# Three to five buffers for messages and one-hot columns, one wait per quad, and first layers two steps apart, in a graph layer on one Trainium2 core

## The chip, the core and the metric

The kernel runs on one core of a Trainium2 chip, in one launch. Its metric is the device time of that launch in microseconds (us). Five engines work side by side, each through its own queue in order, and they wait for one another by semaphores: TensorE (PE, with its weight loads shown as PEld), VectorE (DVE), ScalarE (ACT), GpSimd (POOL) and SyncE (SP). DMA transfers are issued from the queues of SP, ACT and POOL. A wait at the head of a queue holds back all that stands behind it in that queue.

## What is computed

The reference is one layer of a graph network with a layer norm behind it: 12500 nodes of 128 features, 400000 edges sorted by destination, all in 32-bit floats.

```python
rbf = jnp.exp(-(distances[:, None] - centers) ** 2 / (2.0 * width * width))
cut = 0.5 * (jnp.cos(jnp.pi * distances / CUTOFF) + 1.0) * (distances <= CUTOFF)
W = (jax.nn.silu(rbf @ fw1 + fb1) @ fw2 + fb2) * cut[:, None]
messages = (h[src] @ pw + pb) * W
agg = jax.ops.segment_sum(messages, dst, num_segments=num_atoms)
out = h + (jax.nn.silu(agg @ mw1 + mb1) @ mw2 + mb2)
x = _layernorm(x + out)
```

An edge beyond the cutoff gives nothing. The kernel therefore packs the edges that count into a dense list first, and works on that list.

## The kernel before

The packed list is worked through in 139 **quads** (NL) of 512 edges, four tiles of 128 edges each. Two neighbouring quads are an **oct**. The list is made in seven chunks, by DVE instructions for the most part, which run between the first quads. Meanwhile PE projects all node features to the table `proj` in memory. POOL then gathers the projected rows of the edges' sources, four gathers per quad (L1101), into one of the quad buffers. From quad 70 on, the work on the nodes (second network, residual, norm, store) runs between the quads.

One step q of the main loop (L1595 to L1648) does, in this order of code:

- `message(q)`: one DVE product (L1203) of the second layer's result, in a PSUM bank, with the gathered quad. Its output is a `msg` buffer.
- `second(q + 2)`: PE's second layer for the quad after next, a bias matmul (L1184) and four matmuls (L1187), which read `s` and write a PSUM bank. There are four such banks, and a message sets one free.
- `first(o)` and `silu(o)` in two steps of every four: PE's first layer of a whole oct (L1169, four records) into `ph`, which has one buffer, and ACT's activation from `ph` to `s` (L1175). `octs(q)` says which oct. `s` has three buffers.
- in step 4m+3, `basis(o)` for two octs: on ACT a square (L1153) and an exponential (L1157) into `rbf`, which has two buffers.
- `sum_up(q, msg)`: PE adds the messages up by destination (L1237). Each of the four tiles is multiplied with a one-hot matrix, a column of `hot` in the code's words, into the PSUM tile `sums`.
- `place(q + 1)`: DVE makes the next quad's four one-hot columns (L1216), one instruction for each.
- in some steps `add`: DVE adds earlier sums to the table `aggT` (L1271).

POOL's gathers are paced: a gather of quad q waits until a numbered DVE instruction is done, by the table PACE. So POOL's pace hangs on DVE's.

`own` gives out the buffers of messages and one-hot columns. Quad q has the buffer q % 2 of each kind, and from OWN_4 = 66 the buffer q % 4, with two of each kind in quad buffers that are free by then (OTHERS). So before quad 66 the columns of place(q + 1) overwrite what sum_up(q - 1) read, and each of the four columns waits for its own matmul of that sum.

Some source rows are fetched one by one on ACT's queue (`one_row`, L1077, into `row_sb`), for four quads (BY_ACT). `beside` hides a few of these issues behind each activation.

The integer zeros `zero_i`, 376 words wide, clear the packed list in memory, by DMAs on SP's queue (L229).

Of the kernel before, what the change touches and what calls it, by code (L numbers as in the profile page):

```python
# [21 lines left out]
P = 128  # L22
# [4 lines left out]
W = 128  # L27
# [26 lines left out]
MASK_0 = 4  # L54
LATER = 63, (0, 1, 2, 3, 8, 9, 10, 11, 12)
OTHERS = 4, 5, 6, 7
OWN_4 = 66
DIRECT = 32
FIRST = 16
LISTS = 5  # L60
# [27 lines left out]
TAIL = {80: 4, 84: 4, 88: 2, 90: 2, 92: 2, 94: 2, 96: 2}  # L88
LOAD_AT = {80: 12, 84: 11, 88: 10, 90: 9}
NODES = 70  # L90


@with_exitstack
def kernel(
# [122 lines left out]
    nc.gpsimd.iota(iota_i, pattern=[[1, WS]], base=0, channel_multiplier=0)  # L217
    part_i = keep.tile([P, 1], I32, name="part_i")
    nc.gpsimd.iota(part_i, pattern=[[0, 1]], base=0, channel_multiplier=1)
    zero_i = keep.tile([P, 376], I32, name="zero_i")  # L220
    packed = dram.tile([LISTS, MW], I32, name="packed")

    def clear_packed(k, eng):
        a, b = CLEAR[k:k + 2]
        for i in range(LISTS if k == 0 else 3):
            v = packed[i, a:b].rearrange("(p w) -> p w", p=P)
            for w0 in range(0, (b - a) // P, 376):
                n = min(376, (b - a) // P - w0)
                eng.dma_start(v[:, w0:w0 + n], zero_i[:, :n])  # L229

    aggT = keep.tile([P, N], F32, name="aggT")

    to_clear = [(n0, min(n0 + WS, N)) for n0 in range(0, N, WS)]

# [599 lines left out]
    def unpack(c):  # L834
# [110 lines left out]
        yield 0  # L945
        mine = [q for q in SINGLY if QB[c] <= q < QB[c + 1]]
        if mine:
            at_row = work.tile([64, P], I32, name="at_row", bufs=3)
            nc.vector.tensor_scalar(at_row[:np_], f_src[:, :P], float(4 * H), None, op0=OP.mult)
            for q in mine:  # L950
                p = 2 * (q - QB[c])
                singles[q in BY_ACT].extend((q, e, at_row[p:p + 1]) for e in range(P))
# [78 lines left out]
    d_of, rbf_of, ph_of, t_of, s_of, pu_of, got_of, pa_of, hot_of = ({} for _ in range(9))  # L1031


    row_sb = nc.alloc_sbuf_tensor("row_sb", [P, 5, H], F32).ap()

    def own(q, name, also):

        k = q % (4 if q >= OWN_4 else 2)
        if k > 1:
            return quad_sb[OTHERS[2 * also + k - 2]]  # L1040
        if (name, k) not in own_sb:
            own_sb[name, k] = keep.tile([P, QT, H], F32, name=f"{name}{k}")
        return own_sb[name, k]

    own_sb = {}
    singles, alone, regs, row_at = ([], []), {}, {}, [0.0]
    ROW_SEMS = 3
    row_sem = [[tc.alloc_semaphore(f"rows{k}_{i}") for i in range(ROW_SEMS)] for k in range(2)]
# [16 lines left out]
    def one_row(act):  # L1065

        eng, of, n = (nc.scalar, BY_ACT, ACT_AT_ONCE) if act else (nc.sync, BY_SP, AT_ONCE)
        q, e, i = singles[act].pop(0)
        k = of.index(q)
        if e == 0:  # L1070
            alone[q] = row_sb[:, 3 + k % 2, :] if act else row_sb[:, k % 3, :]
        if e % n == 0:
            _, regs[act] = nc.values_load_multi_w_load_instructions(
                i[:, e:e + n], engines=[eng.engine], min_val=0,
                max_val=(N - 1) * 4 * H, skip_runtime_bounds_check_because=
                "sources are at most N - 1 where they are copied")
        row = eng.dma_start(alone[q][e:e + 1, :].bitcast(U8),  # L1077
                            proj.rearrange("n f -> (n f)").bitcast(U8)[ds(regs[act][e % n], 4 * H)]
                            .rearrange("(o f) -> o f", o=1))
        on_own(row, row_sem[act][k % ROW_SEMS], "rows")  # L1080
# [83 lines left out]
    def first(o):  # L1164

        rbf, n = rbf_of.pop(o)
        ph = ps.tile([P, 2, QE], F32, name="ph", bufs=1)
        for h in range(n):
            nc.tensor.matmul(ph[:, h, :], w1_sb[:2 * KR, h, :], rbf[:2 * KR], start=True, stop=True)  # L1169
        ph_of[o] = ph, n  # L1170
# [40 lines left out]
    def place(q):  # L1211

        hot = own(q, "hot", 1)
        for j in range(QT):
            at = 2 * q + j // 2, slice(j % 2, j % 2 + 1)
            nc.vector.tensor_scalar(hot[:, j, :wide(q)], iota_n[:, :wide(q)], dl[:, at[0], at[1]],  # L1216
                                    cut[:, at[0], at[1]], op0=OP.is_equal, op1=OP.mult)
            gathers()
        hot_of[q] = hot

    def wide(q):

        return WIDE_0 if q < DIRECT // QT else WIDTHS[chunk_of(q)]
# [5 lines left out]
    def sum_up(q, msg, js=range(QT)):  # L1229
        hot = hot_of[q]  # L1230
        if q % 2 == 0 and 0 in js:
            pa_of["two"] = ps.tile([P, 2, 2 * W], F32, name="sums", bufs=2)
        pa = pa_of[q] = pa_of["two"][:, q % 2, :]
        n = QT // windows(q)
        for j in js:
            k = j // n
            nc.tensor.matmul(pa[:, k * W:k * W + wide(q)], msg[:, j, :], hot[:, j, :wide(q)],  # L1237
                             start=(j % n == 0), stop=(j % n == n - 1))

    bases = {}  # L1240

# [346 lines left out]

    def octs(q):

        return q // 4 * 2 + 2 + q % 4


    some, counted = None, []
    for q in range(NL - 7):  # L1595
        while todo and q + 2 >= DIRECT // QT and todo[0] <= chunk_of(min(q + 2, NQ - 1)):
            go_on(todo[0])
        msg = message(q)
        nodes(q)
        most[0] = room(q)  # L1600
        fetches(clock[0], most[0])
        fetches(math.inf, min(NL, q + AHEAD + 1))
        gathers()
        assert fetched[0] > QT * min(NL - 1, q + AHEAD)
        if q >= CLEAR_Q:
            clear()
        if loads_later and q >= 8:
            nc.sync.dma_start(*loads_later.pop(0))
        radials(q // 2 + 5)
        one_by_one()  # L1610
        multiplies(q + 1 + EARLY_X)
        if q + 2 < NL:
            second(q + 2)
        if q % 4 < 2 and 2 * octs(q) < NL:
            first(octs(q))
            silu(octs(q))
        if q % 4 == 3:
            for o in (q // 4 * 2 + 4, q // 4 * 2 + 5):
                if 2 * o < NL and q < NL - 8:
                    basis(o)  # L1620
        sum_up(q, msg)
        now = range(added(q), added(q + 1))
        at_once = len(now) == 2 and wide(now[0]) == wide(now[1]) and windows(now[0]) == windows(now[1])
        if at_once:
            bases_of(list(now))
        else:
            for k in now:
                base_of(k, (0,))
        place(q + 1)
        for k in now:  # L1630
            if not at_once:
                base_of(k, (1,))
            add(k)
        tail(q)
        clock[0] = max(clock[0], there_at[q])
        summed[q] = clock[0] + 0.7
        clock[0] += 2.2 + 0.3 * (windows(q) - 1)
        if q == 0:
            clear_packed(2, nc.sync)
        if todo:  # L1640
            pack_until(max(there_at[q + 1], clock[0] + (PACK_US if known[0] >= QB[3] else EARLY_US)), NC_)
        if NODES - 8 <= q < NODES - 2:
            part_of(*(("mb1", mb1_f) if q < NODES - 5 else ("mb2", mb2_f)), (q - NODES + 8) % 3)
        if not todo and not counted:
            counted.append(q)
            count()
        elif counted and some is None and fetched[0] >= QT * NL and not queue:
            some = nc.values_load(bad_i[0:1, 2:3], min_val=0, max_val=3 * E)  # L1648
# [29 lines left out]
    node_stats(80, last_st[:, 4:])  # L1678
    bases_of(list(range(q, NL)))
    place(q + 1)  # L1680
    for o in (octs(q), octs(q + 1)):
        basis(o)
    add(q)
    normal(1)
# [2 lines left out]
    house(q)  # L1687
    msg = message(q)
    second(q + 2)
    first(octs(q - 1))  # L1690
    silu(octs(q - 1))
    sum_up(q, msg)
    place(q + 1)
    node_stats(84, last_st[:, 8:])
# [5 lines left out]
    house(q)  # L1700
    msg = message(q)
    second(q + 2)
    first(octs(q - 1))
    silu(octs(q - 1))
    sum_up(q, msg)
    node_second(88)
    place(q + 1)
# [189 lines left out]
```

## Time and profile before

| | |
|---|---|
| time, median of three runs | 939.34 us (937.1 to 951.75) |
| the profiled execution's own time | 938.97 us |
| its span in the profile | 937.3 us |
| granted TensorE clock, mean | 0.818 |
| DMA, over the span | 91.30 MB, 97 GB/s |
| PE busy | 661.8 us, 71% of the span |
| DVE busy | 563.3 us, 60% |
| POOL busy | 537.4 us, 57% |
| ACT busy | 402.3 us, 43% |

No engine is busy all the time, and what a change is worth must be read from the waits between engines. In a row of waits, the name after the arrow is the engine and line that came last. Where it says "remote", the wait ended by a semaphore that the profile does not put down to an instruction; where it says "issue", the profile shows nothing that was waited for. In a row of the timeline, the first number is the start in us from the span's start, the second the duration, and the bracket the idle time of that engine before it. The quads' stretches are read from the message rows: quad 12 at 233.4 us, quad 66 at 496.3 us, quad 138 at 924.7 us. So 230 to 492 us is the stretch of the packed chunks with two buffers, and 492 to 930 us that with four.

### The profile page before, as it was taken

What the parts mean: (1) busy time and instruction counts of PE and PEld (TensorE: products, weight loads), DVE (VectorE), ACT (ScalarE), POOL (GpSimd) and SP (SyncE); (2) the same over time, 40 slices, a digit from 0 to 9 for tenths busy, and PEclk for the clock granted to TensorE, in tenths of its full rate; (3) what the DMA queues carried; (4) which work ended last, traced back from release to release, by engine and by line L of the source; (5) the groups of instructions that cost most, each with busy time, mean ns of one, the idle gap of its engine ahead of it and who ended that gap; (6) DMA issues with size and microseconds to landing.
All of it is one profiled execution on the core that took longest, in us unless ns stands there. A gap on an engine that the chain in (4) does not pass through costs nothing. (4 is left out here: it accounts for less than half of the span.)

```text
span 937.3 us, 12780 instructions
## 1 busy us (share of the span) xinstructions
PE 661.8 (71%) x3531; PEld 516.3 (55%) x3531; DVE 563.3 (60%) x1733; ACT 402.3 (43%) x567; POOL 537.4 (57%) x573
## 2 busy tenths in 40 slices
PE   4666746557877766776776987679777675966775
PEld 4565535345656644564554666456565454644554
DVE  8367639726878567757677785455554443632546
ACT  4443713215334444634444435345533642544335
POOL 6356546455656565666666555655576566653661
PEclk9688667859889878978988788788897798877789
DMA  7477412323224222232324223431422342233222
GB/s 244 149 238 215 152 42 72 77 55 83 69 81 122 65 71 78 79 91 77 104 65 138 60 64 80 117 108 55 141 71 65 93 136 69 65 93 94 67 76 75
DMA packets 52199, 91.30 MB, mean 97 GB/s; under 512 B 13376, under 2 KB 19616, under 8 KB 52122
## 3 DMA queue, kind: packets, MB, share of 16 engines
q0 software_dynamic: 17968, 37.03, 15.9%
q1 hardware_dynamic: 22868, 35.09, 11.2%
q10 hardware_dynamic: 11286, 18.31, 6.2%
q8 instruction: 29, 0.48, 0.2%
q14 instruction: 48, 0.39, 0.1%
HBM read 74.59 MB, written 15.79 MB: 96 GB/s over the span
## 5 line engine op out<-in xcount | busy, mean ns | idle before, releaser
L1101 POOL DMA_INDIRECT quad<-proj,srci x409 | 389.4, 952 | 275.8 <-issue 92.5
L1187 PEld LDWEIGHTS bank<-fw_sb,s 128*128 128x128 f32 x1112 | 177.1, 225 | 100.8 <-issue 92.5
L1187 PE MATMUL bank<-fw_sb,s 128*128 128x128 f32 x1112 | 181.2, 310 | 29.9 <-issue 29.7
L1175 ACT ACTIVATE s<-ph 128x1024 f32<-128x1024 f32 x70 | 71.2, 1018 | 260.2 <-remote 121.5
L1169 PE MATMUL ph<-rbf,w_sb 102*128 102x512 f32 x278 | 157.1, 693 | 31.8 <-ACT s L1175 28.5
L1216 DVE TENSOR_SCALAR hot<-iota_n,dl,cut 128x80 f32<-128x80 f32 (+4 forms) x408 | 110.6, 337 | 110.8 <-PE sums L1237 64.2
L1237 PEld LDWEIGHTS sums<-hot,msg 128*128 128x128 f32 x816 | 116.1, 210 | 64.8 <-issue 40.8
L1237 PE MATMUL sums<-hot,msg 128*128 128x80 f32 (+4 forms) x816 | 118.5, 292 | 23.4 <-DVE msg L1203 14.8
L1101 POOL DMA_INDIRECT x<-proj,srci x95 | 90.9, 957 | 63.4 <-DVE hot L1216 22.0
L1271 DVE TENSOR_TENSOR aggT<-aggT,sums 128x80 f32 (+4 forms) x209 | 53.8, 257 | 108.8 <-remote 44.5
L1169 PEld LDWEIGHTS ph<-rbf,w_sb 102*128 102x128 f32 x278 | 55.7, 223 | 80.1 <-issue 43.8
L1184 PE MATMUL bank<-fb_b,ones_b 96*128 96x512 bf16 x139 | 59.8, 430 | 51.7 <-DVE msg L1203 19.7
L350 PEld LDWEIGHTS bank<-pw_sb,xT 128*128 128x128 f32 (+1 forms) x292 | 49.5, 242 | 51.2 <-issue 32.5
L1203 DVE TENSOR_TENSOR msg<-bank,quad 128x512 f32<-128x512 f32 (+1 forms) x78 | 52.9, 678 | 33.5 <-remote 9.7
L1237 PE MATMUL sums<-quad,quad 128*128 128x128 f32 (+3 forms) x296 | 51.7, 319 | 23.3 <-issue 18.3
L1237 PEld LDWEIGHTS sums<-quad,quad 128*128 128x128 f32 x296 | 48.0, 237 | 27.6 <-issue 21.8
L1101 POOL DMA_INDIRECT quad<-in_x_dram,srci x48 | 47.1, 981 | 24.1 <-issue 13.1
L1153 ACT ACTIVATE rbf<-d_sb,rbf_bias,rbf_scale 102x512 f32<-102x512 f32 x70 | 56.2, 803 | 9.2 <-issue 7.2
L350 PE MATMUL bank<-pw_sb,xT 128*128 128x128 f32 (+1 forms) x292 | 50.5, 329 | 8.1 <-ACT xT L1007 4.8
L1175 ACT ACT_TABLE_LOAD x35 | 44.9, 1283 | 23.3 <-issue 22.9
L1157 ACT ACTIVATE rbf<-rbf 102x512 f32<-102x512 f32 x70 | 44.1, 630 | 17.3 <-issue 15.9
L1203 DVE TENSOR_TENSOR quad<-bank,quad 128x512 f32<-128x512 f32 (+2 forms) x40 | 25.6, 641 | 41.7 <-PE bank L1187 14.3
(281 smaller groups left out, 834.4 us busy)
## 6 DMA issues: line engine op xcount, KB each, us to landing
d_sb<-near_d ACTq DMA_DIRECT2D x67, 256.0 KB
x<-in_x_dram SPq DMA_DIRECT2D x46, 256.0 KB
row_sb<-proj ACTq DMA_DIRECT2D x512, 0.5 KB
quad<-proj,srci POOLq DMA_INDIRECT x409
proj<-hp SPq DMA_DIRECT2D x24, 256.0 KB
out_dram<-x SPq DMA_DIRECT2D x22, 256.0 KB
x<-proj,srci POOLq DMA_INDIRECT x95
r_d<-in_edge_weight_dram SPq DMA_DIRECT2D x5, 256.0 KB
```

Source lines behind the costliest of these rows:

```text
L350: nc.tensor.matmul(to[:m, k, :], lT[:, k * P:k * P + m], w, start=False, stop=(k == a + c - 1))
L1101: g = nc.gpsimd.indirect_dma_start(out=got[:, j, :], out_offset=None, in_=proj if table is None else table, in_offset=bass.IndirectOffsetO ...
L1153: a = nc.scalar.activation(rbf[:u], d[:u], AF.Square, bias=rbf_bias[:u], scale=rbf_scale[:u])
L1157: nc.scalar.activation(rbf[:u], rbf[:u], AF.Exp, scale=-1.0 / (2.0 * width * width))
L1169: nc.tensor.matmul(ph[:, h, :], w1_sb[:2 * KR, h, :], rbf[:2 * KR], start=True, stop=True)
L1175: nc.scalar.activation(s[:, :n], ph[:, :n], AF.Silu)
L1184: nc.tensor.matmul(pu, ones_b[:, :P], bias_b["fb2"].rearrange("k j f -> k (j f)"), start=True, stop=False)
L1187: nc.tensor.matmul(pu[:, j * H:(j + 1) * H], s[:, j * P:(j + 1) * P], fw2_sb, start=False, stop=(j == QT - 1))
L1203: nc.vector.tensor_mul(msg[:, a:b, :], pu_of[q].rearrange("p (j f) -> p j f", j=QT)[:, a:b, :], got_of[q][:, a:b, :])
L1216: nc.vector.tensor_scalar(hot[:, j, :wide(q)], iota_n[:, :wide(q)], dl[:, at[0], at[1]], cut[:, at[0], at[1]], op0=OP.is_equal, op1=OP.mult)
L1237: nc.tensor.matmul(pa[:, k * W:k * W + wide(q)], msg[:, j, :], hot[:, j, :wide(q)], start=(j % n == 0), stop=(j % n == n - 1))
L1271: nc.vector.tensor_add(to, to, pa[:, k * W:k * W + wide(q)])
```

## The change

It has three edits that belong to it and a few that make room for them.

1. `own` has three buffers, and from quad 66 (now OWN_5) five. Two of the five are the quad buffers of before.
2. In `place`, only the first of a quad's columns waits for PE, namely for the last matmul that read this buffer (`read_by`). The matmuls that no one waits for one by one no longer signal. With three buffers, place(q + 1) overwrites what sum_up(q - 2) read, one step longer ago.
3. `octs(q)` is q // 2 + 2, and a first layer stands in each even step, 4m and 4m+2, where it stood in 4m and 4m+1. The tail has the same two octs at the same places, by LAST_OCTS.
4. For room, `row_sb` has two buffers where five were laid out (the four quads on ACT used two of them), `at_row` has two where it had three, and `zero_i` is a slice of `aggT`, which is cleared later.

```diff
-OWN_4 = 66
+OWN_5 = 66
+LAST_OCTS = 68, 69
...
-    zero_i = keep.tile([P, 376], I32, name="zero_i")
+    aggT = keep.tile([P, N], F32, name="aggT")
+    zero_i = aggT[:, N - 1000:N - 624].bitcast(I32)
...
-            at_row = work.tile([64, P], I32, name="at_row", bufs=3)
+            at_row = work.tile([64, P], I32, name="at_row", bufs=2)
...
-    row_sb = nc.alloc_sbuf_tensor("row_sb", [P, 5, H], F32).ap()
+    row_sb = nc.alloc_sbuf_tensor("row_sb", [P, 2, H], F32).ap()
...
-        k = q % (4 if q >= OWN_4 else 2)
-        if k > 1:
-            return quad_sb[OTHERS[2 * also + k - 2]]
+        k = q % (5 if q >= OWN_5 else 3)
+        if k > 2:
+            return quad_sb[OTHERS[2 * also + k - 3]]
...
-            alone[q] = row_sb[:, 3 + k % 2, :] if act else row_sb[:, k % 3, :]
+            alone[q] = row_sb[:, k % 2, :]
...
-            nc.vector.tensor_scalar(hot[:, j, :wide(q)], iota_n[:, :wide(q)], dl[:, at[0], at[1]],
-                                    cut[:, at[0], at[1]], op0=OP.is_equal, op1=OP.mult)
+            i = nc.vector.tensor_scalar(hot[:, j, :wide(q)], iota_n[:, :wide(q)], dl[:, at[0], at[1]],
+                                        cut[:, at[0], at[1]], op0=OP.is_equal, op1=OP.mult).ins
+            if id(hot) in read_by:
+                tc.declare_no_dep(i, group="sums", keep=[read_by[id(hot)]] if j == 0 else [],
+                                  reason="a quad's first column waits for the last product")
+                if j == 0:
+                    tc.add_manual_dep(i, read_by[id(hot)].name, mybir.DependencyInfo(
+                        mybir.DependencyClass.Sync, mybir.DependencyReason.DATA))
...
-            nc.tensor.matmul(pa[:, k * W:k * W + wide(q)], msg[:, j, :], hot[:, j, :wide(q)],
-                             start=(j % n == 0), stop=(j % n == n - 1))
+            i = nc.tensor.matmul(pa[:, k * W:k * W + wide(q)], msg[:, j, :], hot[:, j, :wide(q)],
+                                 start=(j % n == 0), stop=(j % n == n - 1)).ins
+            if not tc.in_control_flow:
+                tc.add_to_no_dep_group("sums", i)
+                read_by[id(hot)] = i
...
-        return q // 4 * 2 + 2 + q % 4
+        return q // 2 + 2
...
-        if q % 4 < 2 and 2 * octs(q) < NL:
+        if q % 2 == 0 and 2 * octs(q) < NL:
```

What stands in a row on DVE is the same before and after; only the waits differ. In the third chunk, between quads 24 and 46, DVE's rows of two steps are before (in brackets what a row waits for; `x4` stands for four like it; the rows of L541 to L551 are packing, and `msg`, `hot` and `quad` are buffers):

```order
L541 COPY_PREDICATED r_d<-bank_169,r_d 128x510
L547 TENSOR_SCALAR bank_170<-nodes 128x512
L551 SCALAR_TENSOR_TENSOR nodes<-bank_170,nodes 128x512 [waits DVE_49]
L1203 TENSOR_TENSOR msg_1078<-bank_167,quad_76 128x512 [waits DMASW5_49,DMASW6_49,DMASW4_49,DMASW3_49]
L1216 TENSOR_SCALAR hot_1111<-iota_n,dl,cut 128x80 [waits PE_49] x4
L541 COPY_PREDICATED nodes<-bank_170,nodes 128x508 [waits DVE_49]
L541 COPY_PREDICATED r_d<-bank_170,r_d 128x508
L547 TENSOR_SCALAR bank_167<-nodes 128x512 [waits DVE_49]
L1203 TENSOR_TENSOR msg_680<-bank_168,quad_77 128x512 [waits DMASW2_49,DMASW7_49,DMASW1_49,DMASW0_49]
```

And after, at the same place:

```order
L541 COPY_PREDICATED r_d<-bank_168,r_d 128x510
L547 TENSOR_SCALAR bank_169<-nodes 128x512
L551 SCALAR_TENSOR_TENSOR nodes<-bank_169,nodes 128x512 [waits DVE_49]
L1203 TENSOR_TENSOR msg_1077<-bank_166,quad_76 128x512 [waits DMASW5_49,DMASW4_49,DMASW6_49,DMASW3_49,PE_49]
L1216 TENSOR_SCALAR hot_1110<-iota_n,dl,cut 128x80 [waits PE_49]
L1216 TENSOR_SCALAR hot_1110<-iota_n,dl,cut 128x80 x3
L541 COPY_PREDICATED nodes<-bank_169,nodes 128x508 [waits DVE_49]
L541 COPY_PREDICATED r_d<-bank_169,r_d 128x508
L547 TENSOR_SCALAR bank_166<-nodes 128x512 [waits DVE_49]
L1203 TENSOR_TENSOR msg_679<-bank_167,quad_77 128x512 [waits DMASW2_49,DMASW1_49,DMASW7_49,DMASW0_49,PE_49]
```

Three of the four columns wait for nothing now, and the message has a wait for PE of its own. Before, the columns' wait for a later matmul covered the message's. Over the program, quads whose columns wait for PE go from 62 (each four times) to 55 (each once), and messages that wait for PE from 44 to 95.

On PE the first layer moves. In the steps 84 to 87, before (L1284 and L1285 are a node matmul, `ones_b` the weight load of a bias matmul):

```order
L1169 MATMUL ph<-rbf,w_sb 128x512 x2
L1237 MATMUL sums<-hot_1073,msg_1078 128x80 x4
L1184 LDWEIGHTS ones_b
L1184 MATMUL bank_167<-fb_b,ones_b 128x512
L1187 MATMUL bank_167<-fw_sb,s 128x128 x4
L1169 MATMUL ph<-rbf,w_sb 128x512 x2
L1237 MATMUL sums<-hot_1111,msg_680 128x80 x4
```

And after, from the same first layer on (there L1237 is L1243, and L1284 is L1293):

```order
L1169 MATMUL ph<-rbf,w_sb 128x512 x2
L1243 MATMUL sums<-quad_80,quad_78 128x80 x4
L1184 LDWEIGHTS ones_b
L1184 MATMUL bank_166<-fb_b,ones_b 128x512
L1187 MATMUL bank_166<-fw_sb,s 128x128 x4
L1243 MATMUL sums<-hot_1072,msg_1077 128x80 x4
L1293 LDWEIGHTS mb_b
L1293 MATMUL bank_167<-ones_b,mb_b 128x512
L1294 MATMUL bank_167<-aggT,mw_sb 128x512
L1184 LDWEIGHTS ones_b
L1184 MATMUL bank_169<-fb_b,ones_b 128x512
L1187 MATMUL bank_169<-fw_sb,s 128x128 x4
```

The next row there is the second of the two first layers. It has moved behind the sums of its old step and behind the second layer of the step after. Its oct's activation on ACT stays where it stood among ACT's activations: two activations, then the two bases.

More of the change, by code (lines that the diff above doesn't have):

```diff
@@ L229, in clear_packed @@
                 eng.dma_start(v[:, w0:w0 + n], zero_i[:, :n])
-    aggT = keep.tile([P, N], F32, name="aggT")
     to_clear = [(n0, min(n0 + WS, N)) for n0 in range(0, N, WS)]
@@ L1043, in own @@
         return own_sb[name, k]
-    own_sb = {}
+    own_sb, read_by = {}, {}
     singles, alone, regs, row_at = ([], []), {}, {}, [0.0]
@@ L1680 @@
     place(q + 1)
-    for o in (octs(q), octs(q + 1)):
+    for o in LAST_OCTS:
         basis(o)
@@ L1689 @@
     second(q + 2)
-    first(octs(q - 1))
-    silu(octs(q - 1))
+    first(LAST_OCTS[0])
+    silu(LAST_OCTS[0])
     sum_up(q, msg)
@@ L1702 @@
     second(q + 2)
-    first(octs(q - 1))
-    silu(octs(q - 1))
+    first(LAST_OCTS[1])
+    silu(LAST_OCTS[1])
     sum_up(q, msg)
```

## The prediction

> **What bounds the kernel now.** I read the page's busy times first, then DVE's waits by stretch, then POOL's, then one hold row by row.
>
> ```profile
> PE 661.8 (71%) x3531; PEld 516.3 (55%) x3531; DVE 563.3 (60%) x1733; ACT 402.3 (43%) x567; POOL 537.4 (57%) x573
> L1216 DVE TENSOR_SCALAR hot<-iota_n,dl,cut 128x80 f32<-128x80 f32 (+4 forms) x408 | 110.6, 337 | 110.8 <-PE sums L1237 64.2
> ```
>
> No engine is full, so the time lies in waits. The largest idle sum of DVE in one place stands before the one-hot columns: 110.8 us. Its waits in the stretch of two buffers (230 to 492 us) are these, with total, times and longest:
>
> ```profile
> DVE hot L1216 <- remote: 36.4, 15, 5.1
> DVE hot L1216 <- PE sums L1237: 28.1, 15, 4.1
> DVE hot L1216 <- issue: 3.6, 2, 2.9
> DVE hot L1216 <- PE ph L1169: 1.1, 1, 1.1
> DVE hot L1216 <- PE bank L1187: 0.8, 1, 0.8
> ```
>
> They come to 36.4 + 28.1 + 3.6 + 1.1 + 0.8 = 70.0 us in 34 waits. The same view of 492 to 930 us has one row for the columns, and with four buffers they wait for nothing of PE:
>
> ```profile
> DVE hot L1216 <- issue: 0.9, 2, 0.6
> ```
>
> What each engine does in this stretch and in the last one:
>
> ```profile
> 230.00:492.00 262.00, 191.89 (x1043) 147.81 (x1044) 190.60 (x529) 114.74 (x136) 161.23 (x169) 0.85 0.29 82
> 660.00:930.00 270.00, 194.79 (x1030) 149.43 (x1028) 126.94 (x433) 119.77 (x177) 152.52 (x161) 0.83 0.30 86
> ```
>
> The columns are length, then busy time of PE, PEld, DVE, ACT, POOL, the granted clock and the DMA. In the first row DVE's 190.60 and the columns' 70.0 fill 260.6 of 262 us: there DVE either works or stands before a column. So the kernel's time in this stretch is decided by DVE, and what it waits for there is one place. In the last row DVE is busy for only 47% and the columns are no limit.
>
> Now one hold, in order of time (start, duration, and idle time before it in brackets):
>
> ```profile
> 400.21 0.95 POOL L1101 DMA_INDIRECT x<-proj,srci  x1 [0.30 <-issue]
> 400.43 1.80 PE L1237 MATMUL sums<-hot,msg 128*128 128x112 f32 x8
> 401.65 0.34 DVE L1216 TENSOR_SCALAR hot<-iota_n,dl,cut 128x112 f32<-128x112 f32 x1 [3.37 <-PE sums L1237]
> 403.78 0.34 DVE L1216 TENSOR_SCALAR hot<-iota_n,dl,cut 128x112 f32<-128x112 f32 x1 [1.79 <-remote]
> 404.66 0.58 DVE L1216 TENSOR_SCALAR hot<-iota_n,dl,cut 128x112 f32<-128x112 f32 x2 [0.54 <-remote]
> 405.26 0.95 POOL L1101 DMA_INDIRECT x<-proj,srci  x1 [2.06 <-DVE hot L1216]
> 486.88 0.34 DVE L1216 TENSOR_SCALAR hot<-iota_n,dl,cut 128x112 f32<-128x112 f32 x1 [1.53 <-remote]
> 488.27 0.59 DVE L1216 TENSOR_SCALAR hot<-iota_n,dl,cut 128x112 f32<-128x112 f32 x2 [1.05 <-PE ph L1169]
> 489.70 0.34 DVE L1216 TENSOR_SCALAR hot<-iota_n,dl,cut 128x112 f32<-128x112 f32 x1 [0.85 <-PE bank L1187]
> ```
>
> PE's records say that the eight matmuls ended by 402.2, but the second column starts at 403.78 and the third at 404.66. Each column that goes lets a paced gather go, and PE's next signal is seen after that gather. The columns and the gathers take turns: a place costs not one wait but up to four small ones.
>
> **The change, part by part, against the profiled execution's 938.97 us** (0.37 us under the median of the runs, 939.34; I add nothing for that).
>
> *One wait per place, three buffers, quads 2 to 65.* Three of four columns lose their wait. POOL bounds what that is worth:
>
> ```profile
> POOL quad L1101 <- DVE hot L1216: 25.8, 20, 3.5
> POOL x L1101 <- DVE hot L1216: 20.9, 16, 3.0
> ```
>
> POOL stood 25.8 + 20.9 = 46.7 us before gathers that a column released, in 36 stops of 1.30 us. Of each stop 0.30 us is spent anyway (the rows with [0.30 <-issue]), which leaves 46.7 - 36 x 0.30 = 35.9 us. Since gathers follow one another every 0.95 + 0.30 = 1.25 us and are paced by DVE, DVE cannot gain more than that here. That is the upper end. The lower end is nothing: the message now waits for PE itself (its row in the order has PE_49 where it had none). In PE's order it needs the second layer of its quad, which stands right behind the sums that the first column now waits for, so a held signal stops DVE four columns (4 x 0.337 = 1.3 us) later. Which part goes? In the two holds above, the waits inside a place are 1.79 + 0.54 + 1.05 + 0.85 = 4.23 us of 9.13 in all, 46%. I take that share, 0.46 x 35.9 = **16.5 us**, and count nothing for the first column, whose wait I expect again at the message.
>
> Before 230 us the columns waited 36.1 us in 5 waits:
>
> ```profile
> DVE hot L1216 <- PE sums L1237: 36.1, 5, 14.2
> 210.70 1.14 DVE L1216 TENSOR_SCALAR hot<-iota_n,dl,cut 128x56 f32<-128x56 f32 x4 [12.19 <-PE sums L1237]
> 211.42 0.32 PE L926 MATMUL bank<-ident,f_dl 44*128 44x44 f32 x2
> ```
>
> After such a place DVE comes to rows that need PE's L926, here at 211.42, so of 12.19 us it can move only the columns' 1.14 and a packing row or two: about 2 us. The bounds are 0 and the 36.1; I take **2.0 us**.
>
> *From quad 66.* Five buffers for four change no row's wait, since none waited there: nothing, from both sides.
>
> *First layers two steps apart.* What waits for it now, between 492 and 930 us, and one such place:
>
> ```profile
> PE ph L1169 <- ACT s L1175: 22.1, 7, 5.8
> 604.69 1.02 PE L1237 MATMUL sums<-hot,msg 128*128 128x80 f32 x8
> 605.77 1.05 PE L1187 MATMUL bank<-fw_sb,s 128*128 128x128 f32 x8
> 611.48 1.02 ACT L1175 ACTIVATE s<-ph 128x1024 f32<-128x1024 f32 x1 [8.37 <-remote]
> 612.55 1.22 PE L1169 MATMUL ph<-rbf,w_sb 102*128 102x512 f32 x1 [5.73 <-ACT s L1175]
> ```
>
> PE waited there with the odd oct's first layer because `ph` was not yet read: ACT started 4.7 us after the second layer behind them had ended (606.82). After the change PE has only the step's sums (1.02 us for such a group) before the next second layer needs the same activation. So 7 x 1.02 = 7.1 us is the likely gain, 22.1 the upper end. Against it, the odd oct's activation now comes one step later, with two steps to its second layer where it had three, and with one step to the bases behind it on ACT. That chain is the activation (1.02), a table load (1.28), a square and an exponential:
>
> ```profile
> L1175 ACT ACT_TABLE_LOAD x35 | 44.9, 1283 | 23.3 <-issue 22.9
> L1153 ACT ACTIVATE rbf<-d_sb,rbf_bias,rbf_scale 102x512 f32<-102x512 f32 x70 | 56.2, 803 | 9.2 <-issue 7.2
> L1157 ACT ACTIVATE rbf<-rbf 102x512 f32<-102x512 f32 x70 | 44.1, 630 | 17.3 <-issue 15.9
> ACT s L1175 <- remote: 94.0, 11, 15.8
> ```
>
> The chain is 1.02 + 0.80 + 1.28 + 0.63 = 3.7 us, plus row fetches issued between. The messages of quads 12 and 66 stand at 233.4 and 496.3 us:
>
> ```profile
> 233.44 0.67 DVE L1203 TENSOR_TENSOR msg<-bank,quad 128x512 f32<-128x512 f32 x1
> 496.27 0.68 DVE L1203 TENSOR_TENSOR quad<-bank,quad 128x512 f32<-128x512 f32 x1
> ```
>
> So a step takes 262.9 / 54 = 4.87 us there, and in two steps the chain has room for a hold of about 6 us. The 11 late activations wait 94.0 us, 8.5 each; if half of them are odd octs and miss by 8.5 - 6 = 2.5 us, that is 5.5 x 2.5 = 14 us, the lower end. I take 6.3 us of it, a little under a half, because a hold stops DVE as well and PE is then late anyway. Net **0.8 us** gained.
>
> *The room.* `zero_i` in `aggT` makes the first add wait for SP's DMAs that read the zeros:
>
> ```profile
> 106.94 2.80 SPq L229 DMA_DIRECT2D packed<-zero_i  x6
> 154.50 0.59 DVE L1271 TENSOR_TENSOR aggT<-aggT,sums 128x128 f32 x2
> ```
>
> They are issued by 109.74 us, and the first add comes 44.8 us later: no cost. If that cover were gone, the add would hold messages by as much as the DMAs were late. `at_row` with two buffers is written once per chunk at most, and `row_sb` keeps the two buffers that ACT used: nothing.
>
> Sum: 16.5 + 2.0 + 0.8 = 19.3 us, so 938.97 - 19.3 = 919.7, rounded to **920 us**, about 2% down.
>
> The Trainium skill (TensorE: Matmul & The Clock Gate, "The cost: per-tile semaphore tail") says that increments on completion serialize at about 26 ns each and that one increment on the last matmul is enough. By it three increments fewer in 55 quads are worth 55 x 3 x 26 ns, an estimate of 4 us, where my sum has 16.5. The rows above speak for more than the page: the columns of one place came 2.13 and 0.88 us apart, not 26 ns.
>
> **The rivals.**
>
> *The stall only moves: 935 to 945 us.* The message waits as long as the columns did, since both wait for the same held signal, and POOL does its gathers meanwhile. For it: 51 more messages wait for PE, and in the late stretch, where columns are free, DVE stands at another row just the same:
>
> ```profile
> DVE aggT L1271 <- remote: 44.5, 8, 8.5
> ```
>
> Against it: those are waits of one row per step, without the turns of column and gather. Only the 2.0 and 0.8 remain at most: 938.97 - 2.8 = 936.
>
> *Longer holds, slower: 968 us.* A place that no longer stops at its columns lets up to four gathers run in a row, 5 us, and signals to ACT wait as long. The price is read from the late stretch, where holds are long: 94.0 us of late activations in 438 us, against those of the 262 us before:
>
> ```profile
> ACT s L1175 <- remote: 27.5, 4, 10.5
> ```
>
> At the late rate the early stretch would have 94.0 / 438 x 262 = 56.2, which is 28.7 more: 967.7. It decides from the point where a hold is longer than an activation's slack of two steps, 9.7 us. Against it: POOL needs its idle time before columns today only because DVE is late.
>
> *Larger gain: 896 us.* If the first columns' waits go too, because a sum one step older is nearly always seen, the whole 35.9 us come, with 7.1 of PE's: 938.97 - 43.0 = 896. Against it stands the message's wait.
>
> *The clock: 910 us.* The granted clock was 0.85 in the stretch of two buffers, and the slow and fast matmuls differ by two:
>
> ```profile
> L1169 PE MATMUL ph<-rbf,w_sb x278: 591/592/1222, 103.1 to 910.1; 102*128 102x512 f32 x139
> ```
>
> If shorter gaps raised it to 0.90, PE's 191.89 us would shrink to 181.2, another 10.7 us at most, since DVE decides there: 920 - 10 = 910. The Trainium skill's same page (Part 1, "The HAM clock gate") says that an idle window of about 3.4 us halves the clock. Column waits of 5.1 us at most leave few such windows on PE, so I give it little.
>
> **How the numbers follow.** My forecast (908 to 930) has a chance of 0.38, the moved stall (930 to 948) 0.29, longer holds (948 to 975) 0.17, the larger gain 0.10 and the clock 0.06. The range leaves out the larger gain's far half and most of the longer holds: 896 to 955. Cases of both signs are among these, and the forecast's own range is 908 to 930. A measurement of this kernel tells 2% from no change, that is 920.6 and 958.1. A little over half of the forecast's chance, 0.21, lies under 920.6; with the larger gain and the clock that makes 0.37 for faster. Two thirds of the longer holds' 0.17 lie above 958.1: 0.12, to which I add 0.06 for something unseen, such as the message's fifth semaphore. The rest, 0.45, is within 2%.
>
> **What would show it.** DVE's idle before columns in 230 to 492 us falls from 70.0 to under 35; waits of messages for PE grow, to 15 to 30 us; quad 66's message comes at about 478 us instead of 496; from there to the end the time is as before. PE's wait for ACT at first layers falls from 22.1 to about 15, and a new one for `rbf` appears. The forecast is wrong if message waits take over all of the 70.0, if POOL's gathers stretch the holds, or if the late stretch gives back what the early one gained.

## The result, and the profile after

The changed kernel took 949.92 us (median of 4 runs, 947.84 to 967.18) against 938.22 us (4 runs, 935.11 to 951.75): a ratio of 1.0129, with a 95% interval of 1.0086 to 1.0171. It is 1.3% slower, 30 us over the forecast of 920. The time is inside the range of 896 to 955, but the sign is wrong. The profiled execution took 947.84 us. Ratios and intervals, here and below, are taken from undisturbed runs alone, so they can differ by some tenths of a per cent from the quotient of two medians.

The page after, with the busy times and the groups of the columns, the adds and the messages (L1216 as before, L1280 was L1271):

```profile
PE 672.6 (71%) x3531; PEld 519.9 (55%) x3531; DVE 562.4 (59%) x1733; ACT 403.8 (43%) x567; POOL 535.7 (57%) x573
L1216 DVE TENSOR_SCALAR hot<-iota_n,dl,cut 128x80 f32<-128x80 f32 (+4 forms) x440 | 116.4, 341 | 51.1 <-remote 37.8
L1280 DVE TENSOR_TENSOR aggT<-aggT,sums 128x80 f32 (+4 forms) x209 | 54.0, 259 | 128.6 <-remote 50.3
L1203 DVE TENSOR_TENSOR msg<-bank,quad 128x512 f32<-128x512 f32 (+1 forms) x86 | 58.6, 682 | 50.1 <-remote 19.3
```

The adds and the messages on the page of before:

```profile
L1271 DVE TENSOR_TENSOR aggT<-aggT,sums 128x80 f32 (+4 forms) x209 | 53.8, 257 | 108.8 <-remote 44.5
L1203 DVE TENSOR_TENSOR msg<-bank,quad 128x512 f32<-128x512 f32 (+1 forms) x78 | 52.9, 678 | 33.5 <-remote 9.7
```

The idle time before the columns fell from 110.8 to 51.1 us, as the change meant. DVE's work is the same, so the time went elsewhere: before the adds it rose from 108.8 to 128.6 us, before these messages from 33.5 to 50.1 (the group has 86 of the messages where it had 78). DVE's longest waits in 230 to 492 us say what is new:

```profile
DVE hot L1216 <- remote: 25.6, 6, 6.7
DVE aggT L1280 <- ACT aggT L239: 22.5, 5, 8.1
DVE aggT L1280 <- issue: 8.1, 3, 4.0
DVE msg L1203 <- PE ph L1169: 4.6, 2, 2.5
DVE msg L1203 <- remote: 3.7, 2, 2.3
```

The second row had no counterpart before. L239 is `clear()`: ACT sets a piece of `aggT` to zero, 500 columns at a time, one piece in every step from quad 28 to quad 46. An add writes to a place in `aggT` that is known only at run time, so it waits for the last clear ahead of it. In both programs ten adds wait for ACT; before, no time was lost there. One of them after the change, in order of time:

```profile
386.19 1.02 ACT L1175 ACTIVATE s<-ph 128x1024 f32<-128x1024 f32 x1 [2.06 <-PE bank L1187]
386.26 2.81 ACTq L1077 DMA_DIRECT2D row_sb<-proj  x4
389.11 0.62 ACT L239 ACTIVATE aggT<-iota_n 128x500 f32<-128x500 f32 x1 [1.90 <-issue]
389.76 0.51 DVE L1280 TENSOR_TENSOR aggT<-aggT,sums 128x80 f32 x2 [5.50 <-ACT aggT L239]
390.54 0.94 POOL L1101 DMA_INDIRECT quad<-proj,srci  x1 [5.30 <-DVE aggT L1280]
```

The clear stands in ACT's queue behind an activation of the first layer and the four row fetches that `beside` issues behind it. The activation waits for PE, the clear waits for the activation, the add for the clear, and a gather for the add.

One such add before the change, from the rows of the same two engines: its clear ended at 389.32, 2.0 us before the add came, and the add did not wait.

```profile
386.86 1.02 DVE L1216 TENSOR_SCALAR hot<-iota_n,dl,cut 128x80 f32<-128x80 f32 x4 [4.11 <-remote]
387.11 1.02 ACT L1175 ACTIVATE s<-ph 128x1024 f32<-128x1024 f32 x1 [1.08 <-PE sums L1237]
388.70 0.62 ACT L239 ACTIVATE aggT<-iota_n 128x500 f32<-128x500 f32 x1 [0.56 <-issue]
391.34 0.49 DVE L1271 TENSOR_TENSOR aggT<-aggT,sums 128x80 f32 x2
```

### The profile page after: what moved, and what is told of

Its sections match the earlier page's. It is cut to its first block, busy times and chain, and to the rows that moved or that the text cites. A ratio compares the mean times of both kernels' runs of the same rounds, so it can differ in the third digit from the quotient of the medians.

```text
span 946.3 us, 12788 instructions
## 1 busy us (share of the span) xinstructions
PE 672.6 (71%) x3531; PEld 519.9 (55%) x3531; DVE 562.4 (59%) x1733; ACT 403.8 (43%) x567; POOL 535.7 (57%) x573
## 3 DMA queue, kind: packets, MB, share of 16 engines
q0 software_dynamic: 17968, 37.03, 14.2%
## 5 line engine op out<-in xcount | busy, mean ns | idle before, releaser
L1187 PE MATMUL bank<-fw_sb,s 128*128 128x128 f32 x1112 | 183.4, 313 | 41.7 <-issue 32.4
L1169 PE MATMUL ph<-rbf,w_sb 102*128 102x512 f32 x278 | 165.5, 720 | 27.4 <-issue 15.7
L1243 PEld LDWEIGHTS sums<-hot,msg 128*128 128x128 f32 x880 | 129.7, 216 | 56.6 <-issue 48.1
L1243 PE MATMUL sums<-hot,msg 128*128 128x80 f32 (+4 forms) x880 | 133.3, 297 | 21.3 <-issue 17.2
L1216 DVE TENSOR_SCALAR hot<-iota_n,dl,cut 128x80 f32<-128x80 f32 (+4 forms) x440 | 116.4, 341 | 51.1 <-remote 37.8
L1280 DVE TENSOR_TENSOR aggT<-aggT,sums 128x80 f32 (+4 forms) x209 | 54.0, 259 | 128.6 <-remote 50.3
L1169 PEld LDWEIGHTS ph<-rbf,w_sb 102*128 102x128 f32 x278 | 58.3, 232 | 78.8 <-issue 65.4
L1203 DVE TENSOR_TENSOR msg<-bank,quad 128x512 f32<-128x512 f32 (+1 forms) x86 | 58.6, 682 | 50.1 <-remote 19.3
L1153 ACT ACTIVATE rbf<-d_sb,rbf_bias,rbf_scale 102x512 f32<-102x512 f32 x70 | 56.3, 804 | 13.7 <-issue 11.8
L350 PE MATMUL bank<-pw_sb,xT 128*128 128x128 f32 (+1 forms) x292 | 49.7, 325 | 4.1 <-ACT xT L1007 3.7
L347 PE MATMUL bank<-pb_b,ones_b 96*128 96x512 bf16 (+2 forms) x38 | 17.3, 456 | 47.0 <-ACT xT L1007 28.8
L1243 PEld LDWEIGHTS sums<-quad,quad 128*128 128x128 f32 x232 | 33.8, 210 | 22.5 <-issue 16.2
```

Source lines behind the costliest of these rows:

```text
L350: nc.tensor.matmul(to[:m, k, :], lT[:, k * P:k * P + m], w, start=False, stop=(k == a + c - 1))
L1153: a = nc.scalar.activation(rbf[:u], d[:u], AF.Square, bias=rbf_bias[:u], scale=rbf_scale[:u])
L1187: nc.tensor.matmul(pu[:, j * H:(j + 1) * H], s[:, j * P:(j + 1) * P], fw2_sb, start=False, stop=(j == QT - 1))
L1203: nc.vector.tensor_mul(msg[:, a:b, :], pu_of[q].rearrange("p (j f) -> p j f", j=QT)[:, a:b, :], got_of[q][:, a:b, :])
L1216: i = nc.vector.tensor_scalar(hot[:, j, :wide(q)], iota_n[:, :wide(q)], dl[:, at[0], at[1]], cut[:, at[0], at[1]], op0=OP.is_equal, op1=OP ...
L1243: i = nc.tensor.matmul(pa[:, k * W:k * W + wide(q)], msg[:, j, :], hot[:, j, :wide(q)], start=(j % n == 0), stop=(j % n == n - 1)).ins
```

## The experiments

The experiments fell on four chips. On two of them, "the fast chips", the kernel before takes 727 us: 726.90 on the chip of e1 to e4, 726.66 on that of e5 to e8. On the other two, "the slow chips", it takes 943.68 us (e9 to e12) and 953.89 us (e13 to e16), near the 938 of the prediction, whose chip is not on record and is counted with them here. What differs between them is told at the end, as far as it was found. Each result is therefore given against the runs of before on its own chip. Theory A is that the loss is the adds' wait for the clears.

### On the fast chips: the parts

**The room alone** (e1_room: the kernel before with `zero_i`, `row_sb` and `at_row` as after).

> The kernel before with the room alone: the zeros as a slice of aggT, two row buffers, two at_row buffers; buffers, waits and first layers as before. Theory A (the loss comes from the adds' wait for ACT's clears of aggT, 22.5 us in the profile after, and not from the room): 938 us within 3, quad 0's message at 113.8 us within 2. Rival B (the 5.7 us that quad 0 is late after the change, and the 9 us at quad 6, come from the aliased zeros): 944 to 948, quad 0 at about 119 us.

Measured: 727.99 us against 726.90, ratio 1.0011 (0.9995 to 1.0028). The room costs nothing that can be seen. The absolute times of the expectation do not fit this chip, so its rival B, a late quad 0, was tried here alone. On the slow chip of e9 to e12 the traces give no sign of it: quad 0's message comes at 117.3 us in e10_before_fewer, which lacks the room, and at 115.4 to 119.0 us in the three that have it.

**Buffers and one wait, without the spacing** (e2_buffers).

```diff
-        return q // 2 + 2
+        return q // 4 * 2 + 2 + q % 4
...
-        if q % 2 == 0 and 2 * octs(q) < NL:
+        if q % 4 < 2 and 2 * octs(q) < NL:
```

> The changed kernel with first layers back in steps 4m and 4m+1: buffers, one wait per quad and room alone. Theory A (adds in step 4m+1 still meet a clear that stands behind the step before's activation, those in 4m+3 no more): about half of the 22.5 us stays, 935 to 943. Rival C (the spacing of the first layers is what costs, the buffers gain as predicted): 920 to 930. Rival D (the message's wait takes the columns' place and nothing is gained): 938 to 942 with message waits over 30 us before quad 66.

Measured: 726.27 us, ratio 0.9989 (0.9978 to 1.0001). No gain and no loss at the end.

**Spacing alone** (e3_spacing: two, then four buffers, four waits).

```diff
-        k = q % (5 if q >= OWN_5 else 3)
-        if k > 2:
-            return quad_sb[OTHERS[2 * also + k - 3]]
+        k = q % (4 if q >= OWN_5 else 2)
+        if k > 1:
+            return quad_sb[OTHERS[2 * also + k - 2]]
...
-            if id(hot) in read_by:
+            if False:
...
-            if not tc.in_control_flow:
+            if False:
```

> The changed kernel with two, then four buffers and a wait at each of the four columns: first layers two steps apart and room alone. Theory A (the columns' wait for the last step's sums covers the clears in step 4m+1; in 4m+3 the clear stands behind the odd oct's activation of one step before): waits of adds for clears of 5 to 10 us, 940 to 946. Rival C (the spacing costs): 946 to 952. Prediction's own term (0.8 us gained): 938.

Measured: 741.21 us, ratio 1.0204 (1.0172 to 1.0237). Against 727 that is 14.3 us lost, by the part for which I had 0.8 us of gain. Adds wait for clears there, and PE for the bases:

```profile
DVE aggT L1280 <- ACT aggT L239: 11.3, 8, 2.9
DVE hot L1216 <- PE sums L1243: 27.3, 14, 6.7
```

```profile
PE ph L1169 <- ACT rbf L1157: 18.5, 15, 3.2
```

**The changed kernel on a fast chip** (e5_after).

> The changed kernel itself, beside the runs of before on the same chip. On the chip of the first four experiments the kernel before takes 727 us and no wait ends late, so a result is read against that chip's own before. If this chip is like that one: theory A (the adds' wait for clears and the activation's place are small there, gathers decide) 727 to 733, as the first layers two steps apart cost 14 us with two buffers (741.21) and three buffers hide that; rival C (spacing costs whatever the buffers) 738 to 745. If it is like the chip of the prediction: 1.3% slower again, near 950.

Measured: 731.57 us against 726.66, ratio 1.0101 (1.0056 to 1.0145). The loss is there as well, so it doesn't need late signals.

**The clears moved** (e4_clear, and e8_clear beside e5_after): two pieces in each even step, ahead of that step's activation, so that the clear stands behind the activation of two steps before. Nothing else of the changed kernel moves.

```diff
-        if q >= CLEAR_Q:
-            clear()
+        if q >= CLEAR_Q and q % 2 == 0:
+            clear(2)
```

> The changed kernel with aggT's pieces cleared two at a time in even steps, ahead of that step's activation on ACT, instead of one in every step. Nothing else moves. Theory A: the adds' 22.5 us for ACT clears fall to under 4, DVE's row of quad 66 comes 12 to 20 us sooner (498 to 506 us), and of this 10 to 20 us are left at the end: 930 to 940. Rival E (the wait only moves to the next held signal of PE): 946 to 950 with more waits of columns or messages for PE.

> The changed kernel with the clears moved, again, so that it stands beside the changed kernel on one chip. Where signals come late: theory A 10 to 20 us under the changed kernel, 930 to 940; rival E the same as the changed kernel within 4. Where they come at once: 725.3 as before, and 2 to 6 under the changed kernel.

Measured: 725.31 us against 726.90, ratio 0.9985 (0.9962 to 1.0008), and 724.34 against 726.66, ratio 0.9963 (0.9946 to 0.9980). The second is 7.2 us under the changed kernel on the same chip, with intervals well apart; I had expected 2 to 6 us. The adds' waits for clears, of e5_after and then of e8_clear:

```profile
DVE aggT L1280 <- ACT aggT L239: 15.6, 8, 5.5
```

```profile
DVE aggT L1280 <- ACT aggT L239: 4.6, 2, 2.8
```

11.0 us of wait went, and 7.2 us of time. Read by the start of a quad's message in the traces, against e1_room, which is level with before (it ran on the other fast chip, where before takes 0.24 us more):

| quad | e1_room, us | e5_after | e8_clear | e7_buf_clear |
|---|---|---|---|---|
| 24 | 212.6 | -7.4 | -6.9 | -7.0 |
| 48 | 303.4 | +4.6 | -6.8 | -11.8 |
| 84 | 448.0 | +14.5 | +2.9 | -2.9 |
| 102 | 536.4 | +1.6 | -1.7 | -3.4 |
| 138 | 712.0 | +2.3 | -1.8 | -3.6 |

Up to quad 24 the buffers gain about 7 us, as forecast in kind. The clears begin at quad 28, and from there the changed kernel loses 12 us to quad 48, which the moved clears do not lose. From 48 to 84 all three fall back by 9 to 10 us, behind the last clear, for a reason that was not sought, and behind 84 the differences shrink in both directions. (The profiled execution of e5_after, 728.71 us, is the shortest of its four, that of e8_clear, 727.85, the longest of its ten, so their traces end closer together than the medians.)

**One wait with two buffers** (e6_onewait), and **buffers with the clears moved, without the spacing** (e7_buf_clear).

> Only one wait per quad, with two, then four buffers and first layers in 4m and 4m+1; room as in the changed kernel. The column waits for the last product of the step before, so only the turns of columns and gathers go. Where signals come late (before near 938): by the prediction's term of 16.5 us, 920 to 925; if the waits just move, 935 to 942. Where they come at once (before near 727): nothing, 726 to 729, since the columns there wait 18.6 us in 8 waits only.

> Buffers and one wait per quad, first layers in 4m and 4m+1, and aggT's pieces cleared two at a time in even steps. Where signals come late: theory A 915 to 932, the prediction's gain without the adds' new wait; theory D (the message takes the columns' wait) 935 to 942. Where they come at once: 722 to 727, as gathers decide.

Measured: e6_onewait 729.60 us, ratio 1.0035 (1.0016 to 1.0053), a little over what I expected: the first column now waits for the last product, and its waits rose from e1_room's 18.6 us in 8 to

```profile
DVE hot L1216 <- PE sums L1243: 32.6, 14, 6.9
```

So a single wait without more buffers costs here. e7_buf_clear 725.43, ratio 0.9992 (0.9981 to 1.0003), as expected: 12 us ahead of e1_room at quad 66, and level at the end. It differs from e2_buffers (726.27 us) in the clears alone. With first layers in 4m and 4m+1 the clears thus cost under 1 us at the end on these chips; the loss needs the spacing as well here.

### On the slow chips

**Spacing with the clears moved** (e9_space_clear: e3_spacing with the diff of the clears).

> First layers two steps apart with two, then four buffers and four waits, as in e3_spacing, but with the clears two at a time in even steps. On a chip where before takes 727: theory A (e3's loss of 14.3 us is in good part the clears, whose waits were 11.3 us in 8) 728 to 735; rival C (the loss is the spacing itself: the bases and activations come late for PE, 18.5 us of waits for rbf) 737 to 742. On a chip where before takes 938: 930 to 940 by A, 944 to 952 by C.

Measured: 939.82 us against 943.68, ratio 0.9985 (0.9943 to 1.0026). With the clears out of the way the spacing costs nothing here. On a fast chip this pair was not tried, so how much of e3's 14.3 us are the clears, and how much the 18.5 us for bases, stays open. Two things on record point to the clears: between the messages of quads 28 and 46 e3's trace takes 81.0 us where e1_room's takes 69.0, and e8_clear, which is no slower than before, still has nearly all of the wait for bases:

```profile
PE ph L1169 <- ACT rbf L1157: 17.7, 16, 3.2
```

**Fewer gathers** (e10, e11, e12). These leave out the fourth gather of every quad from 66 on, so the product reads old data there.

```diff
-            if q in SINGLY and j == 0:
+            if q in SINGLY and j == 0 or q >= 66 and j == 3 and idx is None:
                 continue
```

> The kernel before without the fourth gather of each quad from quad 66 on (73 gathers left out; the product reads what an earlier quad left in that place). 73 gathers at 1.25 us are 91 us of GpSimd's time. Theory F (from quad 66 on, the gathers decide, and whatever was gained or lost before quad 66 is mostly given back to them): the end comes 25 to 60 us sooner than before, until VectorE or TensorE decide. Rival G (other engines decide there too): under 15 us sooner.

> The same 73 gathers left out of the kernel with three, then five buffers, one wait per quad, first layers in 4m and 4m+1 and the clears in even steps. Theory F: its 12 us at quad 66 are kept now, so it ends 8 to 14 us sooner than the kernel before without these gathers, against 1.2 us sooner with them. Rival G: again 1 to 3 us sooner.

> The same 73 gathers left out of the changed kernel. Theory F: the 7 to 14 us that it has lost between quads 28 and 84 are not given back, so it ends 8 to 16 us later than the kernel before without these gathers, against 4.9 us later with them. Rival G: 4 to 6 us later.

Measured, against 943.68: the kernel before without them 861.79 us (0.9128, 0.9025 to 0.9231), the changed kernel 880.02 (0.9366, 0.9314 to 0.9419), buffers with clears moved 864.08 (0.9111, 0.8998 to 0.9224). Leaving out the 73 gathers saves 81.9 us (73 to 92 by the interval), more than I expected, close to the 91 us of GpSimd's time that they take. So gathers set the end behind quad 66; whether it is GpSimd's time or the transfers that the gathers start was not separated. The changed kernel is now 18.2 us behind, a little over what I expected; with all gathers it was 11.7 behind in the first measurement and is 5.5 behind in e13 below. The traces agree: without the gathers it is 18.4 us behind at the message of quad 66 (513.6 against 495.1) and no nearer at the end, while with them 21.7 us at quad 66 shrink to 8.7 at quad 138. The late stretch gives part of an early loss back. The other half of theory F fell: e11 keeps no gain that can be told from the noise of its few runs, and on this chip there is none to keep. In its trace, of its longest execution, the message of quad 66 comes at 504.9 us, 9.7 later than in e10's.

**The four side by side** (e13 to e16), to see whether the clears are the loss where signals come late.

> The changed kernel again, beside the three below. Where before takes near 940: 1.0 to 1.6% slower than before. Where it takes near 727: 0.6 to 1.4% slower.

> The changed kernel with the clears two at a time in even steps. Where before takes near 940: theory A (the clears are the loss) between 1.5% faster than before and equal to it; rival E (another held signal takes their place) 0.8 to 1.5% slower than before. Where it takes near 727: 0.1 to 0.5% faster.

> Buffers and one wait per quad with first layers in 4m and 4m+1 and the clears moved. Where before takes near 940: the prediction's term of 16.5 us would give 1.7% faster; if the message's wait takes the columns' place (33.6 us of such waits in e11), within 0.6% of before. Where it takes near 727: 0.1 to 0.2% faster.

> The same with a clear in every step. Theory A says that the adds then meet a clear behind an activation in step 4m+1 only: 2 to 6 us more than e15_buf_clear where before takes near 940, 0 to 2 us more where it takes near 727.

| against 953.89 us | us | ratio | 95% interval |
|---|---|---|---|
| e13_after | 959.43 | 1.0063 | 1.0020 to 1.0105 |
| e14_clear | 951.69 | 0.9986 | 0.9951 to 1.0022 |
| e15_buf_clear | 954.23 | 1.0031 | 0.9993 to 1.0069 |
| e16_buffers | 961.88 | 1.0111 | 1.0063 to 1.0160 |

Both pairs say the same: with the clears moved the time falls by 7.7 us, in the spacing of after and in that of before. The traces of the slow chips show where. Between the messages of quads 28 and 46, the stretch of the clears, kernels with more buffers and a clear in every step take 100.3 to 105.5 us (after, e12, e13, e16), those with the clears moved 92.0 to 93.8 (e11, e14, e15), and those with two buffers 92.9 to 93.7 (before, e9, e10). So the clears cost 6.6 us (e13 against e14) and 9.1 us (e16 against e15) there, and without them the third buffer gains nothing there.

In e14_clear no add waits for a clear any more; in e16_buffers, whose first layers stand as before, three do (DVE's waits in 230 to 492 us):

```profile
DVE msg L1203 <- remote: 29.3, 8, 7.6
DVE aggT L1280 <- ACT aggT L239: 13.0, 3, 10.6
DVE hot L1216 <- remote: 12.8, 5, 4.4
```

One of the three is 10.6 us long. So the spacing isn't needed for the loss on this chip; more buffers and one wait are enough, which I read as DVE's earlier arrival at its adds. In e15_buf_clear, where one add waits 1.3 us for a clear, the same stretch has

```profile
DVE hot L1216 <- remote: 23.6, 7, 6.7
DVE msg L1203 <- remote: 14.2, 5, 5.0
DVE msg L1203 <- PE sums L1243: 5.7, 2, 4.6
```

where before had 70.0 us at the columns: part of that is still there, part stands at the messages now. The intervals of each pair touch or nearly do, so the 7.7 us are likely and not sharp. My expectation of 1.0 to 1.6% for e13_after was missed (0.63%), that of 2 to 6 us between e16 and e15 too (7.7). With the clears moved, nothing is left of the predicted gain: 0.9986 and 1.0031.

TensorE's clock does not explain the loss. PE was busy for 10.8 us more in the profile after, at 0.815 against 0.818; but in e14's trace it is busy longer still, 684.5 us at 0.799, and the stretch of the clears takes 93.8 us against 93.6 before.

## Why the prediction was wrong

1. **"The lower end is nothing"** (of the 16.5 us for the columns). This is the step that failed: the term was a loss, and the bound under it did not hold. I asked only which wait for PE comes next, the message, and set the lower end at zero. The adds' wait for ACT's clears was in the program before, met at once, because the columns held DVE until sums of the step before were seen; by then ACT had its activation behind it. With the sum of one step older DVE is at the add sooner and pays for ACT's queue: 22.5 us in the profile, 7.2 and 7.7 us of the time in the experiments that move the clears. That the columns' wait was the cover is argued from the order; that the clears are the loss is shown. The 16.5 us themselves did not come either: with the clears moved, e14 and e15 are level with before.
2. **"whose wait I expect again at the message"** was right, and went further than I allowed: on the slow chips messages wait where they did not (29.3 us in e16, 14.2 + 5.7 in e15; in the profile after 4.6 + 3.7 + 1.8 = 10.1 us, under the 15 to 30 that I named). Most of those in e15 and e16 are "remote", and a message waits for gathers as well as for PE, so that they are waits for PE is likely and not shown. The rival "The stall only moves" (936 us, 0.29) is nearest to what the slow chips do once the clears are out of the way: e14 and e15 lie within 0.4% of before.
3. **"2.0 us" before 230 us** had the wrong sign on the slow chips. From the message of quad 0 to that of quad 6 their traces with four waits take 71.6 us (before), 72.6 (e10) and 73.1 (e9), those with one wait 75.5 (after) to 80.5 (e13). The wait of 14.2 us at the columns moved to a packing row behind PE's L926, as I had said one would, and the longest one there, 14.5 us, is as long:

```profile
DVE dl L933 <- PE bank L931: 20.5, 2, 14.5
```

The rest of the loss in the profile after stands at a later packing row that waits for PE, in 111 to 230 us of before and then of after:

```profile
DVE at_f L535 <- PE bank L752: 4.9, 1, 4.9
```

```profile
DVE at_f L535 <- PE bank L752: 9.6, 1, 9.6
```

Why that wait grew wasn't tried. On the fast chips the same stretch takes 48.7 to 49.7 us with three buffers and one wait, and 49.2 in e1_room.

4. **The spacing, net "0.8 us" gained**. PE's 22.1 us for `s` at first layers went, and a wait for `rbf` came, as the prediction said: 5.8 us in the stretch of 492 to 930 us,

```profile
PE ph L1169 <- ACT rbf L1157: 5.8, 5, 1.9
```

But I had counted behind the moved activation only the bases and, without a price, the row fetches between; the clear that stands behind them in ACT's queue I left out. Alone on a fast chip the spacing costs 14.3 us.

5. **The room, "nothing"**, was right (e1_room, 1.0011). But **"from there to the end the time is as before"** was wrong: the message of quad 66 came at 518.0 us, 21.7 late instead of 18 early, and that of quad 138 at 933.4, only 8.7 late. Of the 21.7 us, 10.3 were there at quad 28, before the clears of the loop begin (5.7 of them at quad 0, where before itself came 3.5 us later in e10's trace). Another 11.9 came between quads 28 and 46. So the stretch of the clears holds about half of what was lost early. The late stretch is set by gathers and gives back most of what comes before it, loss or gain.
6. **The rule on single increments**, an estimate of 4 us by the Trainium skill (TensorE: Matmul & The Clock Gate, "The cost: per-tile semaphore tail"), can't be told from nothing here: e6_onewait, which has the single increment and a later release of the first column, was 0.35% slower.

## What to carry to other kernels

Before a wait is taken away, list every wait that its engine meets behind it up to the next wait for the same engine, those that cost nothing today too: a wait that is met at once may be met at once only because of the one that goes. Here the adds' 0 us became 22.5. When an instruction moves in a queue, look at what that queue holds right behind it, here a clear of 0.6 us that VectorE needed, and put such work ahead of the instruction that can be late. A gain in an early stretch is worth only what the late stretch lets through.

## What the runs showed of the hardware

The same kernel takes 727 us on two chips and 938 to 954 us on others. The engines' work is the same: the page of e1_room, which is level with before (its lines are one lower), has

```profile
PE 591.4 (81%) x3531; PEld 466.3 (64%) x3531; DVE 561.2 (77%) x1733; ACT 401.8 (55%) x567; POOL 537.6 (74%) x573
L1100 POOL DMA_INDIRECT quad<-proj,srci x409 | 389.1, 951 | 124.7 <-issue 56.1
L1174 ACT ACTIVATE s<-ph 128x1024 f32<-128x1024 f32 x70 | 71.2, 1017 | 141.9 <-PE ph L1168 141.7
```

A gather takes 951 ns there and 952 here, DVE is busy for 561.2 us there and 563.3 here; PE's 591.4 against 661.8 goes with a granted clock of 0.920 against 0.818 (661.8 x 0.818 / 0.920 = 588). What differs besides is where the engines wait. In the profile before, ACT's activations waited 121.5 us in 15 waits that the profile puts down to no instruction ("remote"). I read them as signals of PE that are seen late, since in the one laid out in the prediction ACT started 4.7 us after PE's second layer had ended. On the fast chips the activation follows its matmul (`PE ph`) and no such wait occurs. There the gathers follow one another 0.30 us apart nearly all the time (the two largest of POOL's waits, whole span),

```profile
POOL quad L1100 <- issue: 60.6, 199, 0.3
POOL quad L1100 <- DVE hot L1215: 12.5, 41, 0.3
```

and DVE waits for what they bring (`DVE msg L1202 <- DMA quad<-proj,srci: 50.6, 26, 3.6`). I had taken the late signals for a property of the kernel; they go with the chip, or with the state that it was in. What makes them late was not found.
